# A fused attention and gated feed-forward layer: another plan for the work behind the score loop, and the shift rows computed on other engines

## The chip, the cores and the metric

The kernel runs on one core of a Trainium2 chip. The metric is the device time of one execution in microseconds (us), the median of several runs. A core has engines that run side by side, each with its own in-order queue: TensorE (PE; its weight loads are listed as PEld), VectorE (DVE), ScalarE (ACT), GpSimd (POOL) and SyncE (SP), which here issues all DMAs. They wait for one another by semaphores. TensorE writes to PSUM[...]; operands come from SBUF.

## The reference

For each of 8 sequences of 2048 tokens with 512 features, after a layer norm:

```python
xn = layernorm(x)
q = (xn @ Wq.T + bq).reshape(B, M, 8, 8); k = (xn @ Wk.T + bk).reshape(B, M, 8, 8)
v = (xn @ Wv.T + bv).reshape(B, M, 8, 64)
scores = einsum('bmhd,bnhd->bhmn', q, k) / sqrt(8)
scores = where(scores >= 0, scores, 0.2 * scores)
s = gamma * einsum('bhmn,bnhd->bmhd', softmax(scores), v) + xn
base = xn @ W.T
proj = l2norm(xn @ Wp.T + bp)
lw = softmax(proj @ l2norm(sim) * exp(min(temp, CLAMP_MAX)))
ret = where(arange(4) == argmax(lw), lw, 0)          # one of four experts
res = sum_e ret[e] * (xn @ Wd_e.T) @ Wu_e.T          # ranks 1, 2, 4, 8
out = x + s * silu(base + res)
```

All of it is in float32.

## The kernel before

**The score loop.** A batch is cut into 4 blocks of 512 tokens and 4 pairs of heads; a pair of heads on one block of queries is an index s, 16 to a batch, 128 in all. For each s the loop runs over 16 chunks of 128 keys (index i), so there are 2048 steps. In a step (lines 954 to 995) TensorE first subtracts the row maximum from the current scores by a two-row matmul (less_max, L626), then makes the next step's scores (score, L609), then takes the maximum over raw scores of a later s, 25 chunks ahead (max_unit, L561; VectorE reduces it at L568). ScalarE takes the exponential of the current scores (exp, L637, into one of seven ex buffers) and the leaky slope of the next ones (leaky, L619). GpSimd adds the exponentials up (add_up, L669) for the softmax's divisor. TensorE weighs the values with a chunk's exponentials (weigh, L649). Chunks not yet weighed wait in the list last; k is how many a step weighs.

**The work behind the loop.** A generator, back, yields everything else in small pieces, and background() (L775) takes pieces in each step. project_block(b, n) (L334) transposes a block of the normalized input, makes its queries and keys (4 matmuls, L247; split_keys stores them to memory) and its values (16 matmuls, L254, in four groups; store_values). lift_block(b, n) (L382) makes the gate's projection (pps, 4 matmuls), its squares (pw, L395 and L396) and norms (nps), the down projections (dps, 4), the gate (gps, rps) and the output of the feed-forward (zps, 16 matmuls in four groups, each ended by a fifth, L488). A batch's order is lift 1, lift 2, next batch's project 0 and 1, lift 3, project 2 and 3, next batch's lift 0.

Two further generators stand ahead of back: shift_rows(s) (L570), which turns the row maxima into the two rows that less_max subtracts, and ending(s) (L671), which divides by the sums, multiplies by the feed-forward's output and stores. Each takes a step or more for pieces on TensorE: cps (L590), dps2 (L694, written to a tile that the profile also calls dps), atp (L711).

**The plan.** A piece tells its cost in us of TensorE by spend(); a matmul of 512 columns counts MM = 0.86. A yield tells what may follow: HOLD (inside an accumulation), WAIT (another engine has to finish first; the next piece costs no TensorE time or little), FREE, IDLE (let a step pass), SLOW (ScalarE and VectorE have extra work). The list tasks (L727 to 744) gives each block a due time in units of s, and due_at() turns it into the cost that should have been spent by now, with END = 1.45 for each s's ending and shift rows. background() starts a piece of back only if the plan is behind its due cost, and stops after `most` us; with pairs a second matmul follows the first. After a SLOW piece the next step weighs one chunk first.

**Keys and values of the next batch.** load_stacks(s + 2) is called at i = 0. For a new batch it first calls background(force=True) until project_block of block 3 has appended the batch to ready, which happens after its values are stored. load_values(s + 1) is called at i = 6.

Of the kernel before, what the change touches and what calls it, by code (L numbers as in the profile page):

```python
# [8 lines left out]
FP = mybir.dt.float32  # L9
# [3 lines left out]
ALU = mybir.AluOpType  # L13
# [19 lines left out]
def fused_layer_kernel(  # L33
# [111 lines left out]

    hi_bits = filled("hi_bits", HI_BITS, I32)
    minus_one = filled("minus_one", -1.0)
    ln_eps = filled("ln_eps", LN_EPS)

    kst = []  # L150
# [89 lines left out]
    def spend(cost):  # L240
        spent[0] += cost

    def project(ps, wt, xnT):
        for c in range(NC):
            if c:
                yield HOLD
            nc.tensor.matmul(ps, lhsT=wt[:, c, :], rhs=xnT[c], start=(c == 0), stop=(c == NC - 1))  # L247
            spend(MM)

    def token_major(ps, wt, xnT, t, more=False):  # L250
        for c in range(NC):
            if c:
                yield HOLD
            nc.tensor.matmul(  # L254
                ps,
                lhsT=xnT[c][:, t * 128 : (t + 1) * 128],
                rhs=wt[:, c, :],
                start=(c == 0),
                stop=(c == NC - 1 and not more),
            )  # L260
            spend(MM)

    def columns(*tiles):
        return [a[:, c, :] for a in tiles for c in range(a.shape[1])]

    normed = {}
    ready = []
    lifted = []
    fetched = {}

# [63 lines left out]
    def project_block(b, n, following, prefetch):  # L334
# [27 lines left out]
        split_keys(b, n, ps, hi, lo)  # L362
        nc.sync.dma_start(out=XN[b][n], in_=xn)
        nc.sync.dma_start(out=XT[b][n], in_=xnT)
        yield FREE

        vb = one.tile([128, NPAIR, NT, 128], FP, name="vb")
# [13 lines left out]

    def lift_block(b, n, following, prefetch, cols=None):  # L382

        early = cols is not None
        if not early:
            if (b, n) not in fetched:
# [4 lines left out]

        ps = bank([128, BLK], "pps")
        yield from project(ps, wp_sb, cols)
        pw = one.tile([128, 2, BLK], FP, name="pw")
        nc.vector.tensor_scalar(pw[:, 0, :], ps, bp_sb, None, ALU.add)  # L395
        nc.scalar.activation(pw[:, 1, :], ps, AF.Square, bias=bp_sb)  # L396
        yield FREE
        nps = bank([128, NT], "nps")
        for t in range(NT):
            nc.tensor.matmul(  # L400
                nps[:, t : t + 1],
                lhsT=pw[:, 1, t * 128 : (t + 1) * 128],
                rhs=ones[:, 0:1],
                start=True,
                stop=True,
            )
# [13 lines left out]
        for t in range(NT):  # L420
            nc.tensor.matmul(
                gps[:, t, 0:NEXP],
                lhsT=pw[:, 0, t * 128 : (t + 1) * 128],
                rhs=simn,
                start=True,
                stop=True,
            )
# [243 lines left out]
    def ending(s):  # L671
# [54 lines left out]
    A1, A2 = 20 * MM + 2.0, 24 * MM + 3.7  # L726
    tasks = [(lift_block, 0, 0, 16 * MM + 1.7, 1.4)]  # L727
    for b in range(B):
        order = [(lift_block, b, 1)]
        if b + 1 < B:  # L730
            order += [(lift_block, b, 2), (project_block, b + 1, 0), (project_block, b + 1, 1)]
            order += [(lift_block, b, 3), (project_block, b + 1, 2), (project_block, b + 1, 3)]
            order += [(lift_block, b + 1, 0)]
        else:
            order += [(lift_block, b, 2), (lift_block, b, 3)]
        costs = [A2 if f is lift_block else A1 for f, _, _ in order]
        t0 = tasks[-1][4]
        steady = sum(costs) - (costs[-1] if b + 1 < B else 0.0)
        t1 = SEQ * b + (AHEAD if b + 1 < B else LAST)
        run = 0.0  # L740
        for k, (f, bb, n) in enumerate(order):
            run += costs[k]
            end = t0 + (t1 - t0) * run / steady if run <= steady + 0.01 else SEQ * (b + 1.0)
            tasks.append((f, bb, n, costs[k], end))

    def due_at(h):
        w, t = h * END, 0.0
# [3 lines left out]
        return w  # L751

    def behind():
        for k, (f, b, n, _, _) in enumerate(tasks):
            g, bb, nn = (tasks[k + 1] if k + 1 < len(tasks) else (None, 0, 0))[:3]
# [16 lines left out]

    PAIR = 0.5

    def background(force=False, most=MOST, pairs=True):  # L775


        def go(j):
# [11 lines left out]
        while spent[0] < begun + most:  # L790
# [18 lines left out]
    with tc.manual_schedule():  # L809
# [144 lines left out]
        for s in range(B * SEQ):  # L954
            for i in range(CH):
                if i == 0:
                    load_stacks(s + 2)
                if i == 6:
                    load_values(s + 1)
                due[0] = due_at(s + (i + 1) / CH)  # L960
                u = s * CH + i + CH + LEAD
# [9 lines left out]
                    leaky(sc1)  # L971


                begun = spent[0]
                k = 1
                if last and (slow[0] or last[0][1] == CH - 1):
# [67 lines left out]
```

## Time and profile before

| | |
|---|---|
| median of 3 runs | 5834.28 us (5829.07 to 5840.97) |
| the profiled execution | 5841.93 us |
| its span, first to last instruction | 5840.2 us |
| PE busy | 5433.9 us (93%) |
| PEld busy | 1780.7 us (30%) |
| POOL busy | 4705.6 us (81%) |
| ACT busy | 4276.0 us (73%) |
| DVE busy | 3620.9 us (62%) |
| DMA, share of 16 engines | 33.6% |

The main loop runs from 132.5 us (first less_max) to the end. Busy shares are averages over the span, and a busy TensorE isn't one at its peak, since the ends of pipelined matmuls are modelled. Groups of instructions that bear on the change, with their count, busy time and mean:

```profile
L669 POOL TENSOR_TENSOR acc<-acc,ex 128x1024 f32<-128x1024 f32 x1792 | 4236.9, 2364 | 353.0 <-ACT ex L637 268.3
L568 DVE TENSOR_REDUCE mxr<-mx 128x2 f32<-128x1024 f32 x2048 | 2504.2, 1223 | 1814.3 <-PE mx L561 1798.2
L637 ACT ACTIVATE ex<-sc 128x1024 f32<-128x1024 f32 x2048 | 2097.6, 1024 | 1388.2 <-PE sc L609 1198.7
L619 ACT ACTIVATE sc<-sc 128x1024 f32<-128x1024 f32 x2048 | 2086.2, 1019 | 19.9 <-PE sc L609 19.9
L583 POOL TENSOR_TENSOR c<-big,ml 128x8 f32<-128x8 f32 x128 | 26.1, 204 | 186.8 <-ACT ml L582 178.8
```

A line gives source line, engine, operation, the tile written and the tiles read, shapes and count, then busy us and mean ns, then the engine's idle time just before these instructions and what ended most of it. ScalarE's two passes fill 4184 us; before each exponential it waited 0.68 us in the mean (1388.2 over 2048).

### The profile page before, as it was taken

What the parts mean: (1) busy time and instruction counts of PE and PEld (TensorE: products, weight loads), DVE (VectorE), ACT (ScalarE), POOL (GpSimd) and SP (SyncE); (2) the same over time, 40 slices, a digit from 0 to 9 for tenths busy, and PEclk for the clock granted to TensorE, in tenths of its full rate; (3) what the DMA queues carried; (4) which work ended last, traced back from release to release, by engine and by line L of the source; (5) the groups of instructions that cost most, each with busy time, mean ns of one, the idle gap of its engine ahead of it and who ended that gap; (6) DMA issues with size and microseconds to landing.
All of it is one profiled execution on the core that took longest, in us unless ns stands there. A gap on an engine that the chain in (4) does not pass through costs nothing.

```text
span 5840.2 us, 74003 instructions
## 1 busy us (share of the span) xinstructions
PE 5433.9 (93%) x26242; PEld 1780.7 (30%) x26242; DVE 3620.9 (62%) x4716; ACT 4276.0 (73%) x4915; POOL 4705.6 (81%) x2519
## 2 busy tenths in 40 slices
PE   7899999999999999999999999999999999988888
PEld 3333333333333333333333333333333333322222
DVE  5566656666566666666666666666666666555552
ACT  2677767777777777777777777777777777767666
POOL 1788878888888888888888888888888888878777
PEclk9999999999999999999999999999999999988885
DMA  5233333334224242243423434233342334322221
GB/s 200 90 109 121 105 115 88 108 106 152 89 75 152 77 152 86 75 143 95 135 82 95 132 104 130 82 104 123 104 124 89 104 111 129 97 62 80 70 76 33
DMA packets 517991, 614.04 MB, mean 105 GB/s; under 512 B 30780, under 2 KB 429116, under 8 KB 481528
## 3 DMA queue, kind: packets, MB, share of 16 engines
q1 hardware_dynamic: 517624, 609.32, 33.6%
q8 instruction: 209, 3.42, 0.2%
q14 instruction: 158, 1.29, 0.1%
HBM read 405.79 MB, written 201.33 MB: 104 GB/s over the span
## 4 chain that ended last, share of the span: by engine, by line
PE 68%; ACT 21%; DVE 5%; POOL 2%; issue 2%; DMA 1%; SPq 1%; ACTq 0%; POOLq 0%; DVEq 0%
PE av L649 22%; PE sc L626 14%; ACT ex L637 10%; ACT sc L619 9%; PE zps L254 9%; PE vps L254 8%; PE mx L561 5%; PE dps L247 2%; PE pps L247 2%; PE qkps L247 2%; DVE mxr L568 2%; POOL acc L669 1%; ACT xn L292 1%; PE sc L609 1%; DVE bs L277 1%
## 5 line engine op out<-in xcount | busy, mean ns | idle before, releaser
L669 POOL TENSOR_TENSOR acc<-acc,ex 128x1024 f32<-128x1024 f32 x1792 | 4236.9, 2364 | 353.0 <-ACT ex L637 268.3
L568 DVE TENSOR_REDUCE mxr<-mx 128x2 f32<-128x1024 f32 x2048 | 2504.2, 1223 | 1814.3 <-PE mx L561 1798.2
L637 ACT ACTIVATE ex<-sc 128x1024 f32<-128x1024 f32 x2048 | 2097.6, 1024 | 1388.2 <-PE sc L609 1198.7
L649 PE MATMUL av<-ex,v_sb 128*64 128x512 f32 x8192 | 2228.5, 634 | 0.9 <-DVE avs L676 0.9
L619 ACT ACTIVATE sc<-sc 128x1024 f32<-128x1024 f32 x2048 | 2086.2, 1019 | 19.9 <-PE sc L609 19.9
L626 PE MATMUL sc<-shift,ones_r 2*128 2x512 f32 x4096 | 1055.6, 507 | 301.6 <-ACT sc L619 294.3
L609 PE MATMUL sc<-q_sb,k 32*128 32x512 f32 x4096 | 1044.8, 506 | 0.0
L626 PEld LDWEIGHTS sc<-shift,ones_r 2*128 2x128 f32 x4096 | 393.9, 185 | 2050.2 <-ACT sc L619 1947.2
L561 PE MATMUL mx<-k,q_sb 32*128 32x512 f32 x4096 | 831.5, 400 | 13.5 <-DVE mxr L568 13.5
L649 PEld LDWEIGHTS av<-ex,v_sb 128*64 128x64 f32 x8192 | 437.9, 138 | 954.9 <-issue 928.6
L669 POOL TENSOR_TENSOR acc<-ex 128x1024 f32<-128x1024 f32 x128 | 301.9, 2358 | 397.6 <-ACT ex L637 397.6
L254 PE MATMUL zps<-w_sb,xnT 128*128 128x512 f32 x1024 | 567.4, 656 | 12.1 <-DMA xnT<-XT 12.0
L254 PE MATMUL vps<-wv_sb,xnT 128*128 128x512 f32 x960 | 508.3, 633 | 6.8 <-DVE vb L322 2.3
L561 PEld LDWEIGHTS mx<-k,q_sb 32*128 32x128 f32 x4096 | 400.3, 190 | 35.3 <-DVE mxr L568 33.9
L609 PEld LDWEIGHTS sc<-q_sb,k 32*128 32x128 f32 x4096 | 386.6, 186 | 0.8 <-issue 0.8
L254 PEld LDWEIGHTS zps<-w_sb,xnT 128*128 128x128 f32 x1024 | 168.3, 195 | 254.0 <-issue 194.8
L254 PEld LDWEIGHTS vps<-wv_sb,xnT 128*128 128x128 f32 x960 | 153.8, 189 | 210.9 <-issue 176.5
L492 DVE SCALAR_TENSOR_TENSOR g<-th,zps 128x512 f32<-128x512 f32 x128 | 88.0, 688 | 166.9 <-ACT th L491 166.9
L583 POOL TENSOR_TENSOR c<-big,ml 128x8 f32<-128x8 f32 x128 | 26.1, 204 | 186.8 <-ACT ml L582 178.8
L247 PE MATMUL pps<-xnT,wp_sb 128*128 128x512 f32 x256 | 142.1, 646 | 5.6 <-DVE vb L322 5.5
L247 PE MATMUL dps<-xnT,wd_sb 128*128 128x512 f32 x256 | 146.3, 661 | 0.1
L247 PE MATMUL qkps<-xnT,wqk_sb 128*128 128x512 f32 x240 | 123.4, 640 | 2.5 <-ACT xnT L842 1.4
(121 smaller groups left out, 2558.8 us busy)
## 6 DMA issues: line engine op xcount, KB each, us to landing
v_sb<-VS SPq DMA_DIRECT2D x127, 1024.0 KB
k<-KS SPq DMA_DIRECT2D x256, 256.0 KB
XN<-xn SPq DMA_DIRECT2D x32, 1024.0 KB
q_sb<-QS SPq DMA_DIRECT2D x256, 128.0 KB
xnT<-XT SPq DMA_DIRECT2D x32, 1024.0 KB
GS<-g SPq DMA_DIRECT2D x32, 1024.0 KB
gs<-GS SPq DMA_DIRECT2D x128, 256.0 KB
xs<-in_x_dram SPq DMA_DIRECT2D x128, 256.0 KB
```

What stands on the lines that cost most here:

```text
L247: nc.tensor.matmul(ps, lhsT=wt[:, c, :], rhs=xnT[c], start=(c == 0), stop=(c == NC - 1))
L254: nc.tensor.matmul(ps, lhsT=xnT[c][:, t * 128 : (t + 1) * 128], rhs=wt[:, c, :], start=(c == 0), stop=(c == NC - 1 and not more),)
L277: nc.vector.bn_stats(bs, xt[:, t, :])
L492: nc.vector.scalar_tensor_tensor(g[:, t, :], th, 1.0, ps, ALU.add, ALU.mult)
L561: nc.tensor.matmul(mx[:, e, :], lhsT=q_sb[r, t * 128 : (t + 1) * 128], rhs=k_sb[r, kb // 2 * BLK : (kb // 2 + 1) * BLK], start=True, stop= ...
L568: nc.vector.reduce_max(mxr[s][:, :, t, kb : kb + 1], mx, axis=AX.X)
L609: nc.tensor.matmul(sc[:, e, :], lhsT=k_sb[r, i // 2 * 128 : (i // 2 + 1) * 128], rhs=q_sb[r, :], start=True, stop=True,)
L619: nc.scalar.activation(sc, sc, AF.Prelu, alpha=SLOPE)
L626: nc.tensor.matmul(sc[:, e, :], lhsT=ones_r[r, :], rhs=shifts[s][r, :], start=False, stop=True, skip_group_check=True,)
L637: nc.scalar.activation(ex, sc, AF.Exp, scale=qscale)
L649: nc.tensor.matmul(avt[s][64 * e : 64 * e + DV, :], lhsT=v_sb[:, i, 64 * e : 64 * e + DV], rhs=ex[:, e, :], start=(i == 0), stop=(i == CH ...
L669: nc.gpsimd.tensor_tensor(acc[s], old, ex, ALU.add)
```

## The change

- **Plan.** New due times: the next batch's last block is split, its keys due at 13.8 and its 16 value matmuls at 15.0, lift 0 of the next batch at 1.3 of that batch; the rest evenly between. In the last batch all is due at 13.5.
- **Alternation.** background() gets light: it then takes only pieces in state WAIT. The loop sets it, outside the last batch, if more than one chunk waits and either more than three wait or the plan is less than 2.0 us late. The bound of 0.8 us with four waiting chunks goes.
- **Halves.** In the last batch's lifts 1 to 3 each 512-column matmul of project and token_major is made as two of 256 columns, with a yield between.
- **Keys before values.** ready is appended when the keys are stored; a new list, valued, when the values are. load_values waits for valued, and comes as soon after i = 6 as that holds, at i = 13 at the latest.
- **Shift rows.** Three ScalarE operations are replaced by two on VectorE and three on GpSimd.
- **Smaller ones.** pw becomes two tiles, and the squares are issued before the sum. ending waits two steps less.

```diff
@@ project (token_major in the same manner)
         for c in range(NC):
-            if c:
-                yield HOLD
-            nc.tensor.matmul(ps, lhsT=wt[:, c, :], rhs=xnT[c], start=(c == 0), stop=(c == NC - 1))
-            spend(MM)
+            for part in pieces():
+                if c or part.start:
+                    yield HOLD
+                nc.tensor.matmul(
+                    ps[:, part],
+                    lhsT=wt[:, c, :],
+                    rhs=xnT[c][:, part],
+                    start=(c == 0 and part.start == 0),
+                    stop=(c == NC - 1 and part.stop == BLK),
+                )
+                spend(MM / len(pieces()))
@@ project_block
         nc.sync.dma_start(out=XT[b][n], in_=xnT)
+        if n == NB - 1:
+            ready.append(b)
         yield FREE
...
         if n == NB - 1:
-            ready.append(b)
+            valued.append(b)
@@ lift_block
+        fine[0] = b == B - 1 and n > 0
...
-        pw = one.tile([128, 2, BLK], FP, name="pw")
-        nc.vector.tensor_scalar(pw[:, 0, :], ps, bp_sb, None, ALU.add)
-        nc.scalar.activation(pw[:, 1, :], ps, AF.Square, bias=bp_sb)
+        pw = one.tile([128, BLK], FP, name="pw")
+        pw2 = one.tile([128, BLK], FP, name="pw2")
+        nc.scalar.activation(pw2, ps, AF.Square, bias=bp_sb)
+        nc.vector.tensor_scalar(pw, ps, bp_sb, None, ALU.add)
@@ load_values
+        while b not in valued:
+            background(force=True)
@@ shift_rows
-        nc.scalar.activation(ml, m[:, :, 0], AF.Prelu, alpha=SLOPE)
...
-        nc.scalar.activation(big, ml, AF.Copy, scale=-4097.0)
-        nc.scalar.activation(ml, ml, AF.Copy, scale=-1.0)
+        nc.vector.tensor_scalar(big, m[:, :, 0], 0.0, SLOPE, ALU.min, ALU.mult)
+        nc.vector.tensor_scalar_max(m[:, :, 0], m[:, :, 0], 0.0)
+        nc.gpsimd.tensor_tensor(ml, m[:, :, 0], big, ALU.add)
+        nc.gpsimd.tensor_tensor(big, ml, splitter.to_broadcast([128, 2 * NT]), ALU.mult)
+        nc.gpsimd.tensor_tensor(ml, ml, minus_one.to_broadcast([128, 2 * NT]), ALU.mult)
@@ ending
-        for _ in range(2):
-            yield IDLE
         while (b, n) not in lifted:
@@ tasks
-    AHEAD = 13.4
-    LAST = 13.2
+    A1, A2, LIFTED, KEYED, VALUED = 20 * MM + 2.0, 24 * MM + 3.7, 1.3, 13.8, 15.0
+    LAST = 13.5
...
+        total = sum(o[3] for o in order) - (16 * MM if b + 1 < B else 0.0)
+        t0, run = SEQ * b + LIFTED, 0.0
+        for f, bb, n, cost in order:
+            run += cost
+            at = min(run / total, 1.0) * ((KEYED if b + 1 < B else LAST) - LIFTED) + t0
+            if run > total + 0.01:
+                tasks.append((f, bb, n, cost - 16 * MM, at))
+                tasks.append((None, bb, n, 16 * MM, SEQ * b + VALUED))
+            else:
+                tasks.append((f, bb, n, cost, at))
+        if b + 1 < B:
+            tasks.append((lift_block, b + 1, 0, A2, SEQ * (b + 1) + LIFTED))
@@ background
+    LATE, MUCH = 2.0, 3
...
+            if light and state[j] != WAIT:
+                break
@@ the loop
-                if i == 6:
+                if i >= 6 and s + 1 not in vts and (where(s + 1)[0] in valued or i == 13):
                     load_values(s + 1)
...
-                    background(most=MOST if len(last) < 4 else 0.8, pairs=s < (B - 1) * SEQ)
+                    pairs = s < (B - 1) * SEQ
+                    light = pairs and len(last) > 1 and (len(last) > MUCH or due[0] - begun < LATE)
+                    background(pairs=pairs, light=light)
```

pieces() returns two slices of 256 columns while fine[0] is set, else one of 512.

More of the change, by code (lines that the diff above doesn't have):

```diff
@@ L147, in fused_layer_kernel @@
     minus_one = filled("minus_one", -1.0)
+    splitter = filled("splitter", -4097.0)
     ln_eps = filled("ln_eps", LN_EPS)
@@ L241, in spend, with pieces @@
         spent[0] += cost
+    fine = [False]
+    def pieces():
+        if fine[0]:
+            return [slice(0, BLK // 2), slice(BLK // 2, BLK)]
+        return [slice(0, BLK)]
     def project(ps, wt, xnT):
         for c in range(NC):
-            if c:
-                yield HOLD
-            nc.tensor.matmul(ps, lhsT=wt[:, c, :], rhs=xnT[c], start=(c == 0), stop=(c == NC - 1))
-            spend(MM)
+            for part in pieces():
[9 more added lines that the diff above has]
+                spend(MM / len(pieces()))
     def token_major(ps, wt, xnT, t, more=False):
         for c in range(NC):
[L252 to L261, printed above, removed]
+            for part in pieces():
+                if c or part.start:
+                    yield HOLD
+                nc.tensor.matmul(
+                    ps[:, part],
+                    lhsT=xnT[c][:, t * 128 : (t + 1) * 128],
+                    rhs=wt[:, c, part],
+                    start=(c == 0 and part.start == 0),
+                    stop=(c == NC - 1 and part.stop == BLK and not more),
+                )
+                spend(MM / len(pieces()))
     def columns(*tiles):
@@ L267, in fused_layer_kernel @@
     ready = []
+    valued = [0]
     lifted = []
@@ L401, in lift_block @@
                 nps[:, t : t + 1],
-                lhsT=pw[:, 1, t * 128 : (t + 1) * 128],
+                lhsT=pw2[:, t * 128 : (t + 1) * 128],
                 rhs=ones[:, 0:1],
@@ L422, in lift_block @@
                 gps[:, t, 0:NEXP],
-                lhsT=pw[:, 0, t * 128 : (t + 1) * 128],
+                lhsT=pw[:, t * 128 : (t + 1) * 128],
                 rhs=simn,
@@ L720, in ending @@
         yield FREE
-    AHEAD = 13.4
-    LAST = 13.2
-    A1, A2 = 20 * MM + 2.0, 24 * MM + 3.7
-    tasks = [(lift_block, 0, 0, 16 * MM + 1.7, 1.4)]
+    A1, A2, LIFTED, KEYED, VALUED = 20 * MM + 2.0, 24 * MM + 3.7, 1.3, 13.8, 15.0
+    LAST = 13.5
+    tasks = [(lift_block, 0, 0, 16 * MM + 1.7, LIFTED)]
     for b in range(B):
-        order = [(lift_block, b, 1)]
+        order = [(lift_block, b, 1, A2), (lift_block, b, 2, A2)]
         if b + 1 < B:
-            order += [(lift_block, b, 2), (project_block, b + 1, 0), (project_block, b + 1, 1)]
-            order += [(lift_block, b, 3), (project_block, b + 1, 2), (project_block, b + 1, 3)]
-            order += [(lift_block, b + 1, 0)]
-        else:
[L735 to L744, printed above, removed]
+            order += [(project_block, b + 1, 0, A1), (project_block, b + 1, 1, A1), (lift_block, b, 3, A2)]
+            order += [(project_block, b + 1, 2, A1), (project_block, b + 1, 3, A1)]
+        else:
+            order += [(lift_block, b, 3, A2)]
+        total = sum(o[3] for o in order) - (16 * MM if b + 1 < B else 0.0)
[10 more added lines that the diff above has]
+            tasks.append((lift_block, b + 1, 0, A2, SEQ * (b + 1) + LIFTED))
     def due_at(h):
@@ L753, in behind @@
     def behind():
-        for k, (f, b, n, _, _) in enumerate(tasks):
-            g, bb, nn = (tasks[k + 1] if k + 1 < len(tasks) else (None, 0, 0))[:3]
+        jobs = [t for t in tasks if t[0]]
+        for k, (f, b, n, _, _) in enumerate(jobs):
+            g, bb, nn = (jobs[k + 1] if k + 1 < len(jobs) else (None, 0, 0))[:3]
             following = norm(bb, nn) if g is project_block else iter(())
@@ L773, in fused_layer_kernel, with background @@
     PAIR = 0.5
-    def background(force=False, most=MOST, pairs=True):
+    LATE, MUCH = 2.0, 3
+    def background(force=False, most=MOST, pairs=True, light=False):
         def go(j):
```

## The prediction

> **What bounds the kernel now.** I read the page's busy shares and slices first, then the chain of waits, then TensorE's timeline in a quiet stretch, and last the stretches with their granted clock.
>
> ```profile
> PEclk9999999999999999999999999999999999988885
> ...
> PE 68%; ACT 21%; DVE 5%; POOL 2%; issue 2%; DMA 1%; SPq 1%; ACTq 0%; POOLq 0%; DVEq 0%
> ```
>
> The chain runs over TensorE for 68% of the span and over ScalarE for 21%; nothing else matters. Why both, the timeline of TensorE in batch 4 shows (start, length, line, operation). A step of the main loop begins with its first L626.
>
> ```profile
> 3052.88 0.50 PE L626 MATMUL sc<-shift,ones_r 2*128 2x512 f32 x2 [0.47 <-ACT sc L619]
> ...
> 3053.53 1.98 PE L254 MATMUL zps<-w_sb,xnT 128*128 128x512 f32 x4
> 3055.49 0.50 PE L626 MATMUL sc<-shift,ones_r 2*128 2x512 f32 x2
> ...
> 3056.14 1.12 PE L254 MATMUL zps<-w_sb,xnT 128*128 128x512 f32 x2
> 3057.20 1.08 PE L649 MATMUL av<-ex,v_sb 128*64 128x512 f32 x4
> 3058.21 0.50 PE L626 MATMUL sc<-shift,ones_r 2*128 2x512 f32 x2
> ...
> 3058.86 1.13 PE L254 MATMUL zps<-w_sb,xnT 128*128 128x512 f32 x2
> 3059.43 0.79 PE L488 MATMUL zps<-wu_sb,dst 128*128 128x512 f32 x1
> 3060.15 1.08 PE L649 MATMUL av<-ex,v_sb 128*64 128x512 f32 x4
> 3061.16 0.50 PE L626 MATMUL sc<-shift,ones_r 2*128 2x512 f32 x2
> ```
>
> Two background matmuls and no chunk of values take 2.61 us (3052.88 to 3055.49). One matmul and one chunk, the same arithmetic, take 2.72: the switch of kind costs 0.11. One matmul, L488 and a chunk take 2.95. A step can't be shorter than about 2.61 either way, because exp L637 and the leaky step L619 follow L626 in turn on ScalarE; steps that only carry a small transpose measure 2.61 too.
>
> I cut the whole trace at these L626 and sorted the steps by their TensorE work. Batches 1 to 6 (1536 steps; total 202 us over 2.61 a step), median and sum over 2.61:
>
> | step | count | median us | over 2.61, us |
> |---|---|---|---|
> | 1 matmul + 1 chunk | 526 | 2.73 | 77 |
> | 2 chunks | 219 | 2.62 | 10 |
> | 2 matmuls | 183 | 2.62 | 13 |
> | 1 matmul + L488 + 1 chunk | 60 | 2.96 | 21 |
> | 2 matmuls + L488 | 36 | 2.81 | 12 |
> | small piece + 1 chunk | 456 | 2.61 to 2.76 | 38 |
> | 1 chunk alone | 50 | 2.62 | 2 |
> | forced, at the end of s = 13 | 6 | 7.41 | 29 |
>
> Batch 0 is 70 us over, 27.5 of it in one forced step of 30.1; batch 7 is 78 over. The opening (132 us) and the tail (15) complete the span. The forced step:
>
> ```profile
> 3585.80 1.98 PE L254 MATMUL vps<-wv_sb,xnT 128*128 128x512 f32 x4
> ...
> 3588.57 1.98 PE L247 MATMUL pps<-xnT,wp_sb 128*128 128x512 f32 x4 [0.78 <-DVE vb L322]
> 3590.48 0.50 PE L626 MATMUL sc<-shift,ones_r 2*128 2x512 f32 x2
> ```
>
> load_stacks(16) drains the next batch's last values before it may read the keys, and the scores stand still.
>
> Batch 7 is another matter. Its stretches s = 2 to 13 and s = 13 to the end (busy by engine, then granted clock):
>
> ```profile
> 5178.00:5682.00 504.00, 439.29 (x2074) 133.47 (x2072) 282.30 (x340) 355.16 (x404) 395.35 (x201) 0.89 0.22 69
> 5710.00:5754.00 44.00, 44.00 (x153) 11.39 (x149) 19.00 (x19) 27.18 (x29) 33.49 (x17) 0.50 0.15 48
> 5682.00:5840.00 158.00, 139.01 (x492) 35.48 (x492) 47.84 (x60) 95.73 (x104) 112.10 (x54) 0.58 0.16 50
> ```
>
> The clock halves, and of batch 7's 78 us, 68 fall in steps that it touches. There a bare step takes 3.05, one with a matmul 5.0.
>
> **The change, part by part.** The sum is made against the profiled execution, 5841.9 us (span 5840.2), 0.13% over the median 5834.3; I take 8 off at the end.
>
> *Pairs.* With light, a step with two or three chunks waiting leaves the background alone and weighs two; with one waiting, it takes two matmuls. Both kinds measure 2.62. Counted in slots (a chunk, a matmul or a piece), a batch needs 256 + 176 + 76 = 508 of the 512 that 256 steps hold, so pairs must carry nearly everything, and can. Of the 526 mixed steps, the 132 of zps partly stay: after each SLOW step the rule still takes one chunk and one matmul, and leaves the block's fourth matmul alone with L488. The other 394 (54 us over) become pairs (8 over): 46 gained. Of zps's 65 us in all (23 + 9 + 21 + 12) I give a third, 22, as half the blocks should align; bounds 5 and 40. Batch 0 (some 60 mixed steps) gives 8, batch 7's 54 mixed and 12 L488 steps 10 if halves replace them. Together 86.
>
> *Keys first.* ready now comes 16 matmuls earlier. Before, at s = 14 the old order had everything but three of those 16; so keys are ready by ten matmuls if progress stays. But the due line is flatter (0.68 us of background a step to 13.8, against 0.78 in batch 0 and 0.70 later), and planned idleness is lost for good: 508 slots of 512 leave four to waste, and every step with one chunk alone wastes one (8 a batch before). Forced matmuls equal waste less four, at about 0.95 each wherever they fall. Bounds in batches 1 to 6: 0 and 29; I take 15. In batch 0 the old order was short of the keys by four transposes and four matmuls, about 7 us, so 20 of 27.5 goes.
>
> *New wait.* load_values may force until valued. It stands at i = 13 of s = 15, 13 steps after the values are due, so it costs nothing unless the plan is 9 us late; up to 5 us a batch then. SP holds only the values' load there and the chunks of the next s behind it; the load issues in 0.38 us.
>
> *Shift rows.* ScalarE loses three instructions of 0.19 to 0.21, 128 times: 78 us busy. Worth: 0 to 78. They start behind L619 and fit the gap of 0.68 us (1388 us over 2048) in which ScalarE waits for L626 anyway, and steps with them measure the usual 2.73. I take 0. VectorE gets two tiny ones, priced by the 128x8 reduce L574 at 0.19: 49 us in an engine 62% busy. GpSimd gets three more of 0.20 (78 us), and its first now waits for VectorE, behind the max L568; but it stops waiting for ScalarE (179 us at L583). Adds are queued behind it, lagging 4.7 us at worst after it now; I take the same lag, bounds minus and plus 1.5. The sums are read over five steps after, so 0. If that cover went, each s would lose up to 1 us.
>
> *Two idle yields less in ending.* Three loads (0.63 us each on SP) and the pieces behind them come two steps earlier, ahead of the shift rows' eight stores instead of after; same work, 0. *Split pw.* Square no longer waits for the add (14 us of wait, 10 times, in front of nps): 2 at most, inside the above.
>
> *Batch 7: halves and the clock.* Three lifts at 0.37 a step give about one half matmul (0.43) in each step up to 13.5. A half step is 0.65 + 0.43 + 0.20 of switch + 1.01 = 2.3 us on TensorE, under 2.61, so the extra instructions cost nothing at full clock. The Trainium skill, *TensorE: Matmul & The Clock Gate* (Part 1), says the clock falls to half after an idle window of some 3.4 us and returns after a busy one. The row disagrees on the cause: in 5710 to 5754 TensorE is busy 44 of 44 us at clock 0.50, and no wait of 3.4 us precedes it; low stretches begin in runs of bare steps (0.66 + 0.86 busy of 2.61). By the rule, halves change nothing here: gain 0. By the row, an even half in each step keeps the share at 75%, where steps with 0.28 to 0.66 of small work mostly held the clock. I follow the row, not fully, since nps, gps and L488 still leave bare steps: of 52 us lost to the clock before s = 13, 32 return. The last 40 steps have no background left and keep their 17.
> The same page (Why this matters for your kernels) asks for all sizes of at least 512, which speaks against halves: each needs its own weight loads. Two loads of 0.195 us (zps row) against 0.43 of streaming hide; if they didn't, 0.4 us for 144 halves, still within the 0.3 spare of a step but for 0.1: 14 us. I take 0.
>
> *Clock in batches 1 to 6.* 28 us were lost there, mostly at s = 0 and 1, after the old plan's slow stretch (0.59 a step). An even 0.66 to 0.72 gives 7.
>
> Sum: 86 + 15 + 20 + 32 + 7 = 160. 5842 - 160 = 5682; less 8 is **5675 us**.
>
> **Rivals.**
> *Pairs only (0.18).* The clock in batch 7 stays low and forced drains stay as long: about 86 - 16 = 70 back, 5765. For it: waste of planned idleness, and half the clock's loss is unexplained. Against: the old order met its values with three matmuls missing.
> *The clock falls at the end of each s (0.07): slower.* Pieces now start only with one chunk waiting, so cps, dps2, atp and a bare step line up in every s; in batches 3 and 6 just such a run, followed by a transpose, halved the clock (a step of 3.82, 1.2 over; a paired step at half clock 4.86, 2.2 over). At 1.8 each, 128 of them cost 230: 5905. It decides from some 90 windows on. Against: only three of twelve such runs did it before.
> *The order does not alternate (0.05).* If the plan runs over 2 us late it fills to four waiting chunks and alternates there; if early, bare steps appear. Then nothing changes: 5830.
>
> **Numbers.** Likeliest 0.70, own range 5610 to 5745 (zps, drains and clock at their ends). For 8 in 10 I reach into pairs only: 5605 to 5780. Within 0.2% (12 us) is what a measurement here can't tell from no change. Faster: 0.70 + 0.18 + little = 0.89; same 0.03; slower 0.08.
>
> **What will show it.** Mixed steps under 250 in batches 1 to 6, steps of two chunks and of two matmuls near 80 each a batch; no step of 7.4 at the end of s = 13, one below 15 in batch 0; clock over 0.95 in s = 2 to 13 of batch 7; waits of POOL's c gone from ScalarE to VectorE; L619 and L637 unchanged. Wrong if steps of 3 to 5 us spread through all batches, or if new forced stretches appear at s = 14 and 15.

## The result, and the profile after

The changed kernel takes 5802.42 us (median of 7 runs, 5799.22 to 5818.58), beside 5834.28 for the kernel before in the same session (7 runs): a ratio of 0.9944, 95% interval 0.9924 to 0.9965. The forecast was 5675 us, range 5605 to 5780: the kernel is faster, but by about 32 us where 160 were summed up. The profiled execution took 5811.92 us (span 5810.2, mean clock 0.966), 30 us less than that of before; the accounts below are made between these two.

The page of the changed kernel, first the granted clock in 40 slices, then the chain of waits by engine, then three groups. (L637 is now L663, L619 is L645, and the first of GpSimd's shift-row operations is L606.)

```profile
PEclk9899999999999999999999999999999999998986
...
PE 63%; ACT 23%; DVE 6%; issue 2%; POOL 2%; DMA 2%; SPq 1%; ACTq 0%; POOLq 0%; DVEq 0%
...
L663 ACT ACTIVATE ex<-sc 128x1024 f32<-128x1024 f32 x2048 | 2095.9, 1023 | 1360.0 <-PE sc L635 1196.0
...
L645 ACT ACTIVATE sc<-sc 128x1024 f32<-128x1024 f32 x2048 | 2088.3, 1020 | 19.8 <-PE sc L635 19.8
...
L606 POOL TENSOR_TENSOR ml<-m,big 128x8 f32<-128x8 f32 x128 | 26.2, 205 | 167.2 <-DVE m L605 167.2
```

ScalarE's two big passes and its wait (1360 us, 1388 before) are much as before. GpSimd still waits 167 us ahead of the shift rows, now for VectorE instead of ScalarE. The step from one less_max to the next tells more. Time over 2.61 us a step, summed, in batches 1 to 6 (a "drain" is the last step of s = 13, in which load_stacks forces work, with the step after it where that is long):

| step, batches 1 to 6 | before: count, us over | after: count, us over |
|---|---|---|
| 1 matmul + 1 chunk | 526, 77.3 | 132, 18.6 |
| 2 chunks | 219, 10.3 | 426, 19.6 |
| 2 matmuls | 183, 12.6 | 366, 21.9 |
| 1 matmul + fifth zps matmul + 1 chunk | 60, 20.9 | 36, 12.4 |
| 2 matmuls + fifth | 36, 12.1 | 60, 12.1 |
| small piece + 1 chunk | 456, 38.3 | 432, 27.0 |
| 1 chunk alone | 50, 2.0 | 72, 0.8 |
| drain | 28.8 | 89.1 |
| all | 202.2 | 201.6 |

The alternation does what it says: mixed steps become pairs. The steps outside the drains take 61 us less here, and the drains give 60 back. What is gained lies in batch 0 (70.0 to 54.9) and batch 7 (78.4 to 64.5).

TensorE's timeline in the changed kernel, batch 4, where s = 13 ends (start, length, line, operation; in brackets the idle time before and its releaser):

```profile
3560.08 0.50 PE L652 MATMUL sc<-shift,ones_r 2*128 2x512 f32 x2
...
3560.75 1.94 PE L675 MATMUL av<-ex,v_sb 128*64 128x512 f32 x8
3563.69 0.66 PE L362 MATMUL tp<-ident,xn 128*128 128x128 f32 x4 [1.00 <-ACT xn L310]
3565.22 1.03 PE L362 MATMUL tp<-ident,xn 128*128 128x128 f32 x4 [0.88 <-DVE xnT L365]
3567.12 1.09 PE L362 MATMUL tp<-ident,xn 128*128 128x128 f32 x4 [0.87 <-DVE xnT L365]
3569.08 1.09 PE L362 MATMUL tp<-ident,xn 128*128 128x128 f32 x4 [0.87 <-DVE xnT L365]
3570.95 5.97 PE L257 MATMUL qkps<-xnT,wqk_sb 128*128 128x512 f32 x8 [0.78 <-DVE xnT L365]
3576.85 0.50 PE L652 MATMUL sc<-shift,ones_r 2*128 2x512 f32 x2
...
3579.12 1.98 PE L271 MATMUL vps<-wv_sb,xnT 128*128 128x512 f32 x4 [1.53 <-DVE lo L326]
3581.04 0.50 PE L652 MATMUL sc<-shift,ones_r 2*128 2x512 f32 x2
```

From L652 to L652 this step lasts 16.77 us. Before, it held three value matmuls of the next batch and two matmuls of the lift behind them (pps), and lasted 7.41. Now the next batch's last block isn't even transposed: four transposes (of four instructions each) go through one PSUM bank, the place that their results are written to, and all but the first wait 0.87 us until VectorE has copied the one before (L365), and then the four key matmuls (eight instructions) take 5.97 us instead of 3.70. The step after it waits 1.53 us for VectorE's split of these keys (L326) and lasts 4.19. Batches 0 to 6 all look like this (14.3 to 16.8 us).

Three stretches of the changed kernel (busy by engine in the order PE, PEld, DVE, ACT, POOL, then granted clock and DMA): this drain, then batch 7 from s = 2 up to the start of s = 13, then the rest of it.

```profile
3564.00:3577.00 13.00, 9.59 (x28) 4.66 (x27) 2.76 (x4) 1.80 (x4) 4.08 (x2) 0.61 0.32 113
...
5150.00:5654.00 504.00, 452.51 (x2238) 161.34 (x2234) 290.33 (x381) 353.28 (x376) 407.01 (x237) 0.89 0.25 70
5654.00:5810.00 156.00, 133.52 (x505) 35.20 (x503) 50.55 (x65) 95.06 (x99) 113.72 (x60) 0.64 0.16 51
```

The clock is 0.61 in the drain. In batch 7 it is 0.89 from s = 2 up to s = 13, as before (0.89), and 0.64 after that (0.58 before).

### The profile page after: what moved, and what is told of

It is laid out like the page before. It is cut to its first block, busy times and chain, and to the rows that moved or that the text cites. A ratio compares the mean times of both kernels' runs of the same rounds, so it can differ in the third digit from the quotient of the medians.

```text
span 5810.2 us, 74735 instructions
## 1 busy us (share of the span) xinstructions
PE 5380.3 (93%) x26386; PEld 1859.1 (32%) x26386; DVE 3656.9 (63%) x4972; ACT 4212.7 (73%) x4531; POOL 4783.6 (82%) x2904
## 4 chain that ended last, share of the span: by engine, by line
PE 63%; ACT 23%; DVE 6%; issue 2%; POOL 2%; DMA 2%; SPq 1%; ACTq 0%; POOLq 0%; DVEq 0%
PE av L675 19%; PE sc L652 14%; ACT ex L663 11%; ACT sc L645 10%; PE zps L271 8%; PE vps L271 8%; PE mx L585 5%; PE qkps L257 2%; DVE mxr L592 2%; PE dps L257 2%; POOL acc L695 2%; PE pps L257 2%; DMA q_sb<-QS 1%; DVE bs L295 1%; PE sc L635 1%
## 5 line engine op out<-in xcount | busy, mean ns | idle before, releaser
L592 DVE TENSOR_REDUCE mxr<-mx 128x2 f32<-128x1024 f32 x2048 | 2502.6, 1223 | 1593.3 <-PE mx L585 1576.5
L663 ACT ACTIVATE ex<-sc 128x1024 f32<-128x1024 f32 x2048 | 2095.9, 1023 | 1360.0 <-PE sc L635 1196.0
L675 PE MATMUL av<-ex,v_sb 128*64 128x512 f32 x8192 | 2170.2, 630 | 0.3
L645 ACT ACTIVATE sc<-sc 128x1024 f32<-128x1024 f32 x2048 | 2088.3, 1020 | 19.8 <-PE sc L635 19.8
L652 PE MATMUL sc<-shift,ones_r 2*128 2x512 f32 x4096 | 1057.1, 505 | 291.0 <-ACT sc L645 279.1
L652 PEld LDWEIGHTS sc<-shift,ones_r 2*128 2x128 f32 x4096 | 397.9, 185 | 2019.5 <-ACT sc L645 1949.1
L675 PEld LDWEIGHTS av<-ex,v_sb 128*64 128x64 f32 x8192 | 458.8, 138 | 809.3 <-issue 784.5
L271 PE MATMUL zps<-w_sb,xnT 128*128 128x512 f32 (+1 forms) x1120 | 541.7, 598 | 14.7 <-DMA xnT<-XT 10.7
L271 PE MATMUL vps<-wv_sb,xnT 128*128 128x512 f32 x960 | 481.7, 622 | 11.3 <-DVE lo L326 10.8
L271 PEld LDWEIGHTS zps<-w_sb,xnT 128*128 128x128 f32 x1120 | 188.5, 192 | 259.3 <-issue 193.9
L606 POOL TENSOR_TENSOR ml<-m,big 128x8 f32<-128x8 f32 x128 | 26.2, 205 | 167.2 <-DVE m L605 167.2
L257 PE MATMUL qkps<-xnT,wqk_sb 128*128 128x512 f32 x240 | 136.1, 703 | 7.5 <-DVE xnT L365 5.5
L257 PE MATMUL dps<-xnT,wd_sb 128*128 128x512 f32 (+1 forms) x280 | 141.1, 620 | 0.0
L257 PE MATMUL pps<-xnT,wp_sb 128*128 128x512 f32 (+1 forms) x280 | 133.3, 588 | 0.3
```

What stands on the lines that cost most here:

```text
L257: nc.tensor.matmul(ps[:, part], lhsT=wt[:, c, :], rhs=xnT[c][:, part], start=(c == 0 and part.start == 0), stop=(c == NC - 1 and part.stop ...
L271: nc.tensor.matmul(ps[:, part], lhsT=xnT[c][:, t * 128 : (t + 1) * 128], rhs=wt[:, c, part], start=(c == 0 and part.start == 0), stop=(c = ...
L592: nc.vector.reduce_max(mxr[s][:, :, t, kb : kb + 1], mx, axis=AX.X)
L645: nc.scalar.activation(sc, sc, AF.Prelu, alpha=SLOPE)
L652: nc.tensor.matmul(sc[:, e, :], lhsT=ones_r[r, :], rhs=shifts[s][r, :], start=False, stop=True, skip_group_check=True,)
L663: nc.scalar.activation(ex, sc, AF.Exp, scale=qscale)
```

## The experiments

Theory D, after the result: the steps are full, so what the background can't fit by s = 14 is forced there, and the price is set by how it is forced. Eleven kernels were run, each beside the kernel before on the same chip. From each profiled execution: the drains of all batches, the mixed steps (1 matmul + 1 chunk) of batches 1 to 6, the time over 2.61 us in steps of batches 1 to 6 that the low clock touches outside the drains, and all of batch 7 (us over 2.61 a step).

| kernel | median us | ratio to before, 95% | drains | mixed | low clock | batch 7 |
|---|---|---|---|---|---|---|
| before | 5834 | | 57 | 77 | 28 | 78 |
| changed | 5802 | 0.9924 to 0.9965 | 105 | 19 | 25 | 65 |
| changed, no pairs | 5987 | 1.0224 to 1.0272 | 99 | 79 | 147 | 84 |
| changed, two banks | 5772 | 0.9864 to 0.9916 | 69 | 19 | 14 | 72 |
| changed, no halves | 5822 | 0.9951 to 0.9982 | 103 | 19 | 19 | 85 |
| changed, shift rows on ScalarE | 5821 | 0.9945 to 0.9979 | 110 | 18 | 33 | 68 |
| before + pairs | 5907 | 1.0085 to 1.0126 | 103 | 12 | 95 | 86 |
| before + keys first | 5853 | 0.9985 to 1.0023 | 31 | 87 | 67 | 84 |
| changed, earlier due times | 5819 | 0.9947 to 0.9983 | 110 | 18 | 31 | 74 |
| changed, dense steps | 5821 | 0.9955 to 0.999 | 11 | 9 | 49 | 60 |
| before + pairs + keys first | 5893 | 1.0063 to 1.0144 | 102 | 17 | 70 | 92 |
| two banks, then weigh | 5779 | 0.988 to 0.9933 | 57 | 19 | 22 | 59 |
| changed, no keys first | 6032 | 1.0329 to 1.0375 | 252 | 17 | 96 | 61 |

The low clock varies between executions of the same code, so a difference of some 10 us in the last two columns is not read. The kernels also ran on different chips; so the ratios are compared, not the medians alone.

**No pairs.** The changed kernel without light.

```diff
-                    background(pairs=pairs, light=light)
+                    background(most=MOST if len(last) < 4 else 0.8, pairs=pairs)
```

> The changed kernel without light: the old rule (1.6 us of background, 0.8 with four chunks waiting), all else as changed. Theory D (pairs worked as predicted, and the forced stretch at s = 14, 14.9 us a batch over the floor in the trace, ate the gain): the mixed steps come back, the forced stretch stays, so some 55 to 75 us slower than the changed kernel: about 5870, slower than before too. Rival P (pairs were worth little, and the gain came from the plan): within 20 us of the changed kernel.

The mixed steps came back as expected (18.6 to 78.7), but the kernel was 185 us slower than the changed one, three times the forecast. The drains stayed (99 us), with the same four transposes and four key matmuls forced, and batches 1 to 6 again had 12 steps each with one chunk alone. So the new drains aren't the work of the pairs: the rest of the change makes them without these. Some 65 us of that are one step in each of batches 1 to 6, at s = 14, of 13.1 to 13.9 us. Its timeline in batch 4 (all engines, most lines left out) shows a wait that no theory had named:

```profile
3682.48 1.30 SPq L329 DMA_DIRECT2D KS<-hi  x2
...
3696.61 1.53 SPq L711 DMA_DIRECT2D xs<-XN  x1
...
3704.27 0.70 DVE L738 TENSOR_TENSOR atp<-atp,xs 128x512 f32<-128x512 f32 x1 [9.42 <-DMA xs<-XN]
...
3704.88 1.21 DVE L592 TENSOR_REDUCE mxr<-mx 128x2 f32<-128x1024 f32 x1
...
3706.15 0.79 PE L585 MATMUL mx<-k,q_sb 32*128 32x512 f32 x2 [8.16 <-DVE mxr L592]
```

SP begins the drain's stores at 3682.48 and issues the ending's load of xs only at 3696.61, after them and the stacks' loads. VectorE stands 9.42 us at L738, the row maxima (L592) are queued behind it, and TensorE's next maximum waits 8.16 us. VectorE waits so 7 times, 65.5 us in all. These steps are among those with a low clock, which cost 147 us outside the drains. In the changed kernel the load is issued as late (15.5 to 16.3 us after the start of s = 14, against 4.3 to 5.1 before), but there it lands 2.6 to 4.0 us before its first use.

**Two banks.** In load_stacks, the forced work alternates between two PSUM banks instead of one.

```diff
-        while b > 0 and b not in ready:
-            background(force=True)
+        if b > 0 and b not in ready:
+            banks[:] = [(ps_m, "m"), (ps_x, "mx")]
+            while b not in ready:
+                background(force=True)
+            banks.clear()
```

> The changed kernel, with two PSUM banks for what is forced at s = 14 in place of one, so that a transpose need not wait for the copy of the one before. Work and order are the same. Theory D: the forced stretch is dear because its four transposes and four copies follow one another through one bank and the clock falls meanwhile; it shrinks from 15 to 16 us to about 10 to 12, 4 to 5 us a batch, so 25 to 40 us faster than the changed kernel: about 5770. Rival (the stretch's length is set by the normalizations on ScalarE, or is hidden by what follows): within 10 us of it.

TensorE's timeline of the drain in batch 4 of the two-bank kernel:

```profile
3524.16 0.50 PE L655 MATMUL sc<-shift,ones_r 2*128 2x512 f32 x2
...
3524.83 1.94 PE L678 MATMUL av<-ex,v_sb 128*64 128x512 f32 x8
3527.79 1.36 PE L362 MATMUL tp<-ident,xn 128*128 128x128 f32 x8 [1.02 <-ACT xn L310]
3529.32 1.33 PE L362 MATMUL tp<-ident,xn 128*128 128x128 f32 x8 [0.17 <-DVE xnT L365]
3531.44 3.70 PE L257 MATMUL qkps<-xnT,wqk_sb 128*128 128x512 f32 x8 [0.78 <-DVE xnT L365]
3535.07 0.50 PE L655 MATMUL sc<-shift,ones_r 2*128 2x512 f32 x2
```

The same work in 10.91 us: the waits of 0.87 become one of 0.17, which saves 2.5 us; the transposes at full speed save 1.2, and the key matmuls, 3.70 instead of 5.97, save 2.3. Of the drains' time over 2.61, 2.8 us lie in steps with a low clock, against 97 in the changed kernel. The drains fell by 37 us and the median by 30. So the bank's turn-around and the clock that falls with it are a third of the drains' price; this kernel is faster than both the one before and the changed one.

**No halves**, and **shift rows on ScalarE**: the changed kernel with one part put back.

```diff
-        fine[0] = b == B - 1 and n > 0
+        fine[0] = False
@@ the other kernel
-        nc.vector.tensor_scalar(big, m[:, :, 0], 0.0, SLOPE, ALU.min, ALU.mult)
...
+        nc.scalar.activation(ml, m[:, :, 0], AF.Prelu, alpha=SLOPE)
+        nc.scalar.activation(big, ml, AF.Copy, scale=-4097.0)
+        nc.scalar.activation(ml, ml, AF.Copy, scale=-1.0)
```

> The changed kernel with whole matmuls in the last batch. Theory D (halves fill steps evenly and saved some clock; the last batch is 14 us shorter in the changed trace, part of it from its plan): 5 to 20 us slower than the changed kernel. Rival H (halves cost weight loads and made the last batch longer than it need be): 5 to 20 us faster.

> The changed kernel with the shift rows back on ScalarE. Theory D: the three operations fit ScalarE's gap, so within 10 us of the changed kernel. Rival S (the longer chain over VectorE and GpSimd delays sums or steps and took gain away): 15 us or more faster. The other way (ScalarE was bound and the move brought the gain): 15 us or more slower.

Without halves batch 7 took 84.5 us over, with them 64.5. Over all profiled executions, those without halves lie at 78 to 92 (five kernels) and those with them at 59 to 74, one at 84 (eight kernels): the means are 17 apart. But four of the five without halves have the old plan too, so the one clean pair is 84.5 against 64.5. With the shift rows on ScalarE every kind of step keeps its time within what the clock moves (mixed steps 18.1, small pieces 20.5). The intervals of both kernels overlap that of the changed one, so in the time itself neither part can be told from nothing.

**Pairs alone**, and **keys first alone**: the kernel before with light and its rule, or with ready ahead of the values. In each the old plan stays.

```diff
@@ pairs alone, in the loop
-                    background(most=MOST if len(last) < 4 else 0.8, pairs=s < (B - 1) * SEQ)
+                    pairs = s < (B - 1) * SEQ
+                    light = pairs and len(last) > 1 and (len(last) > 3 or due[0] - begun < 2.0)
+                    background(pairs=pairs, light=light)
@@ keys first alone, in project_block
+        if n == NB - 1:
+            ready.append(b)
```

> The kernel before with light and its pairs alone (plan, keys, shift rows, halves as before). By the trace mixed steps fall from 526 to about 130 in batches 1 to 6, worth some 60 us there and 5 in batch 0. Theory D (what does not fit the 512 slots of a batch has to be forced): steps with one chunk alone rise, so the matmuls forced at s = 14 rise from 4 to 8 to 10 a batch, at about 1 us each: 30 us given back. About 35 us faster than before: 5800. Rival P (pairs are worth nothing by themselves): within 12 us of before.

> The kernel before with ready after the keys and valued after the values alone. This is the step that the prediction priced at 35 us. Theory D: the order falls behind until the four matmuls of block 3's keys are forced in every batch (3.4 us of plan, about 5 to 7 with the wait for the split), so batches 1 to 6 win nothing, and batch 0 some 20: 5805 to 5825. Rival K (the prediction's step holds, and it was spoilt only by the flatter plan): keys in time, 35 us or more faster: below 5800. Rival L (the later loads of keys and queries are then waited for at i = 7): slower than before.

Pairs alone took the mixed steps from 77 to 12, and made the kernel 1.0 per cent slower: longer drains (13.4 us a batch, 40.7 in batch 0) and a low clock outside them, 95 us against 28. Its TensorE timeline in batch 6 shows how that begins in one place:

```profile
4969.72 0.64 PE L694 MATMUL dps<-acc,ones 128*32 128x256 f32 x8
...
4973.04 0.28 PE L590 MATMUL cps<-ident,c 128*16 128x128 f32 x1 [0.73 <-POOL c L585]
...
4974.91 0.66 PE L711 MATMUL atp<-ident,avs 128*128 128x128 f32 x4
...
4984.72 0.50 PE L626 MATMUL sc<-shift,ones_r 2*128 2x512 f32 x2 [0.88 <-ACT sc L619]
...
4987.34 0.79 PE L626 MATMUL sc<-shift,ones_r 2*128 2x512 f32 x2 [0.88 <-ACT sc L619]
...
4988.49 1.12 PE L344 MATMUL tp<-ident,xn 128*128 128x128 f32 x4
...
4991.44 0.79 PE L626 MATMUL sc<-shift,ones_r 2*128 2x512 f32 x2
```

dps2, cps and atp stand in neighbouring steps; after two steps of two chunks (left out) come two bare ones (4982 and 4985), the less_max pair goes from 0.50 to 0.79, and from then on a step with a transpose takes 4.10. It is much the run of light steps that the prediction's clock rival named. Keys first alone shortened the drains by 26 us (6.3 a batch); 57 us came back at s = 14 and 15 (all batches), where VectorE waited for the same load of xs (21.8 us, 7 times) and the clock fell.

**Earlier due times**, and **dense steps**: the changed kernel with KEYED at 12.6; and with, besides, a chunk weighed beside two matmuls whenever the plan is over 16 us late in s = 4 to 13.

```diff
-    A1, A2, LIFTED, KEYED, VALUED = 20 * MM + 2.0, 24 * MM + 3.7, 1.3, 13.8, 15.0
+    A1, A2, LIFTED, KEYED, VALUED = 20 * MM + 2.0, 24 * MM + 3.7, 1.3, 12.6, 14.6
@@ the other kernel (12.6 and 15.0)
-                    if spent[0] - begun > 1.5 and len(last) < 4:
+                    rush = s % SEQ in range(4, 14) and due[0] - begun > 16
+                    if spent[0] - begun > 1.5 and len(last) < 4 and not rush:
```

> The changed kernel with keys due at 12.6 in place of 13.8 and values at 14.6 in place of 15.0. Theory D (the order is at the capacity of its steps, and due times do not bind): the same transposes and key matmuls are forced at s = 14, within 10 us of the changed kernel. Rival E (the even plan sets the keys too late): the forced stretch goes, 60 us or more faster.

> The changed kernel with keys due at 12.6 and, from s = 4 to 13 of a batch while it is over 16 us late, steps of two matmuls and a chunk (no chunk held back), so that nothing is forced at s = 14. Theory D: the forced stretch (15 us a batch, 105 in all) goes, and 12 dense steps a batch come at about 1 us each, 84 in all: some 10 to 30 us faster than the changed kernel, 5770 to 5795. Rival (the stretch was the whole loss, and the dense steps hide under ScalarE): 80 us or more faster. Rival (dense steps push exponentials back as well): slower than the changed kernel.

Earlier due times changed nothing (drains 110): the keys' due time isn't what holds the work back. Dense steps removed the drains (105 to 11), but 72 dense steps of 3.59 and 3.82 us in batches 1 to 6 cost 78 us, and 12 more in batch 0 12 us. The expected gain of 10 to 30 wasn't there, and the time can't be told from that of the changed kernel: the intervals overlap. So the work that doesn't fit cost 1.08 us for each dense step (77.7 over 72), in sum as much as the drains.

**Pairs and keys first together** on the kernel before, and **two banks, then weigh**, in which the first step of s = 14 weighs two chunks instead of asking for value matmuls at once.

```diff
@@ two banks, then weigh
-                    background(pairs=pairs, light=light)
+                    first = s % SEQ == SEQ - 2 and i == 0 and pairs
+                    background(pairs=pairs, light=light or first)
```

> The kernel before with pairs and keys first alone: the old plan, no halves, shift rows on ScalarE, idle yields kept. Theory D (order at capacity; what doesn't fit is forced at s = 14): the two together mend each other's losses, as pairs give time to the steps and keys first shortens the drain of 13 to 14 us that pairs alone had; the planned forced work is 5.4 a batch, as in the changed kernel, but the plan runs 26 us late at the end of batch 0's s = 13. So the changed kernel's drains (90 to 110 us over all batches), mixed steps below 25 us over in batches 1 to 6, batch 7 at 80 to 86: 5805 to 5830 us. Rival P (the new plan is what keeps the clock and the drains in bounds): drains as with pairs alone, low clock spread over the batches, 5870 or more.

> The two banks kernel, with light set in the first step of s = 14, so that the step after the drain weighs two chunks rather than wait for the keys' split in front of its first value matmul. Theory D: the step of 4.19 that followed each of seven drains becomes one of about 2.6, the drain itself stays 10.6: 7 x 1.6 = 11 us less than two banks, near 5760. Rival Q (the split is waited for one step later just the same, as VectorE is the one behind): the wait moves into the next step, and the time is that of two banks, 5772.

Together on the old plan, pairs and keys first gave 1.0104 of the time before: D's forecast of 5805 to 5830 failed, the rival's held. The drains were those of the changed kernel (102 us), so the 71 us between the two profiled spans (5881.3 and 5810.2) come from elsewhere: 45 from steps of batches 1 to 6 at a low clock outside the drains, 28 from batch 7. The difference to the changed kernel is the new plan, the halves, the shift rows and the smaller parts. Halves act in batch 7 alone and putting the shift rows back changed nothing that can be told, so the 45 us belong to the new plan or to the smaller parts (two idle yields less in ending, the split of pw); no run separates these. They help only beside pairs: without pairs the kernel with all of them (no pairs, 1.0248) is far slower than keys first on the old plan (1.0004), in part by the wait for xs. Two banks, then weigh, removed the step of 4.19 after the drain (drains 69 to 57, as D said), but the time came back within s = 14: the second and the eighth step of it grew by 10 us over the seven batches, and s = 14 and 15 together took 25.7 us over, 24.7 with two banks. Its time can't be told from that of two banks (the intervals overlap). So rival Q was right that the wait moves, if not all of it into the next step.

**No keys first.** The changed kernel with ready appended beside valued again.

```diff
-        if n == NB - 1:
-            ready.append(b)
         yield FREE
...
         if n == NB - 1:
+            ready.append(b)
             valued.append(b)
```

> The changed kernel with keys first alone undone: ready comes again with valued, after the last 16 value matmuls, while the plan still has these due at 15.0. Theory D (what is unfinished at s = 14 is forced, at about 2 us for a planned one): the planned forced work is 20.9 a batch instead of 5.4. A forced stretch of 20.9 planned took 40.7 us in batch 0 of pairs alone, 38 over a step; seven of these are 267, against 105 for the changed kernel's drains: 160 slower than it, 5960 us or so. Rival (keys first is worth the 14 us that lay between pairs alone and pairs with keys first): 5830 us.

The drains were 252 us, near the 267 expected; s = 14 and 15, left without background after them, ran at a low clock and added 61 us more. Two stretches of batch 4, the drain and the bare steps behind it:

```profile
3676.00:3714.00 38.00, 28.24 (x80) 11.72 (x80) 8.14 (x11) 5.44 (x7) 7.64 (x6) 0.91 0.47 170
3740.00:3768.00 28.00, 25.37 (x104) 6.67 (x100) 12.56 (x11) 18.64 (x20) 21.89 (x11) 0.63 0.24 59
```

So keys first is no gain of its own but a condition of the new plan, which has the values due at 15.0: without it the changed kernel is 230 us slower by the medians. On the old plan it made no difference beside pairs (1.0105 without, 1.0104 with).

One count runs through the profiles. The matmuls and transposes forced in a drain, beyond the two slots that its step has anyway, are the steps of the batch with one chunk alone less four: before 8 and 4 forced (batches 2 to 6), keys first alone 8 and 4, pairs and keys first 11 and 7, changed 12 and 8, and dense steps 16 and 12 (as dense steps, not forced). Pairs alone fits less well, with 13 to 15 and 8 to 10. Their price differs (time over, with the long step behind): 1.2 us each before, 1.1 with keys first alone, 1.9 in the changed kernel, 1.2 with two banks.

## Why the prediction was wrong

- **Keys first failed**, the only term with the wrong sign: it was to give 35 us, and the drains took 48 more (57 to 105). The rule "Forced matmuls equal waste less four" held; what went into it, and the price "about 0.95 each wherever they fall", did not. The waste: the prediction took that of before, 8 steps a batch with one chunk alone, for given and hoped for better, so that 2.3 us a batch were to be left in batches 1 to 6, some two or three matmuls. The profile has 12 such steps, hence eight forced pieces. The price: 14.9 us over a batch for the eight, 1.9 each, as four of them were transposes in a chain through one bank, at a clock of 0.61, and the step behind waited for the split. With a second bank the price was 1.2, the split's wait included. Why there are 12 bare steps rather than 8 was not settled: pairs raise them on the old plan (13 to 15 alone, 11 with keys first), and the new plan or the smaller parts raise them without pairs (12).
- **Pairs** were right in kind, high in size. The mixed steps outside zps were to give 46; all mixed steps gave 58.7, and the pairs that replaced them took 18.6, net 40. The prediction priced 394 new pairs at 8 us, by their median of 2.62; its own table has 23 us over for 402 of them, at which rate they cost 22. zps was to give 22; its steps with the fifth matmul gave 8.5. With 11 from the small pieces, batches 1 to 6 gained 61 of the 68 forecast (46 + 22). The 10 of batch 7 go into the next point.
- **Batch 7's halves and clock**: 32, and 10 of pairs, were forecast; 14 came. By the profiles halves help (about 17), which lies between the rule's 0 and the row's 32; but the sign named for the row's reading, a clock over 0.95 in s = 2 to 13, is absent: 0.89, as before. The step that failed is the spreading: of the 192 steps of s = 2 to 13, 42 carry one half, 38 carry two (a whole matmul) and 63 nothing but chunks. An even half in each step was therefore never tried, and whether it would hold the clock stays open.
- **Clock in batches 1 to 6**: 7 forecast, 3 measured (27.8 to 25.0); these 3 are part of the 61 above.
- **Batch 0**: 8 outside the drain forecast, 4 measured; in the drain 20 forecast, about 11 measured (30.1 to 16.0, and a step of 5.38 after it).
- **Shift rows at 0** and the **waits of values at 0** stand: L663 and L645 as before, GpSimd's wait moved to VectorE, and putting the rows back changed nothing that can be told.
- **The rivals.** Pairs only (5765) had the mechanism that came, but not that the drains grow. In time the third rival (5830, no alternation) lay nearer, by chance, since the order did alternate. The clock rival (slower) did not decide here, yet pairs alone ran into it; the prediction took the low clock for a property of pairs, and it turned out to depend on what stands beside them. Of the signs named, the mixed steps came (132, under 250) and the pairs nearly (71 and 61 a batch, near 80 named); the step at the end of s = 13 was to vanish and doubled, and that of batch 0 stayed over 15 (16.0). Forced work at s = 14 was named as a sign of being wrong, and it was the one that came.

In sum (profiles): 64 us less in the other steps of batches 0 to 6, 14 less in batch 7 and 48 more in the drains make the 30 us.

## What to carry to other kernels

When a schedule is near capacity (here 508 of 512 slots, by the prediction's count), cheaper steps gain nothing in the places where unfinished work is forced: count the empty slots that the whole change leaves before pricing what is left. Price forced work as a chain, with its bank, its copies and its clock, not at the rate that the same instructions have inside a full pipeline. Price a step by its mean over the floor, not by its median. Pairs (1.0105), keys first (1.0004) and both together (1.0104) gained nothing on the old plan, and stand in a kernel that gains with the new one, so undoing single parts of a change measures conditions, not shares.

## What the runs showed of the hardware

- In a chain of four transposes with waits of 0.87 us between them TensorE's clock halved at once: the second already ran 1.03 us against 0.66. With one wait of 0.17 instead the clock stayed full (1.00 from 3527 to 3535 in the kernel with two banks), in the same work. The Trainium skill, *TensorE: Matmul & The Clock Gate* (Part 4: PE-mode transpose), says that work in transpose mode doesn't count as busy for the clock in the same way. The profile doesn't show whether these transposes use that mode. Other matmuls are 8.3 us apart in the one drain (3562.69 to 3570.95) and 4.7 in the other (3526.77 to 3531.44), so it could be this as well as the waits; no run here separates the two.
- Being busy did not bring the clock back at once. In pairs alone TensorE was busy 10.00 of 10 us, by the profile, at a clock of 0.53, as this window of batch 6 shows. What ended the low stretch no run shows.

```profile
4995.00:5005.00 10.00, 10.00 (x38) 4.01 (x37) 4.81 (x7) 4.99 (x7) 4.70 (x2) 0.53 0.03 14
```

- A load that SP issues behind a drain's stores comes late because it is issued late: some 16 us into s = 14 instead of 5. From issue to landing it took 6 to 9 us with these stores ahead, and 7.5 to 9 in the kernel before. In the kernel without pairs VectorE waited up to 10.5 us for it (7 times, 65.5 us in all), in keys first alone 21.8 us in all, in the changed kernel not at all.
